# A fused transformer kernel on one core: own start and end for the feed-forward stages, SBUF pools that wait tile by tile, another load order

## The chip, the cores and the metric

The kernel runs as one launch on one NeuronCore of a Trainium2 chip. The metric is the device time of one execution in microseconds (us), taken as the median of several runs. One further execution is recorded by the hardware profiler, and all durations below come from that recording. Engines are named as in the profile: PE is TensorE, PEld its weight loads, DVE is VectorE, ACT is ScalarE, POOL is GpSimd, SP is SyncE, which here only issues DMAs.

## What is computed

The kernel works on x of 8 x 256 x 128 floats (2048 tokens of width 128) and adds six sublayers to it in turn, each on a layernorm of x:

```python
x = x + 0.5 * ffn(layernorm(x))          # a graph of six attention nodes, see below
x = x + attn(layernorm(x))               # 16 heads of 64, rotary, softmax
x = x + 0.5 * ffn(layernorm(x))          # the same graph and weights again
x = x + 0.5 * experts(layernorm(x))      # 8 experts, top 2
x = x + mixer(layernorm(x))              # two state-space scans and an FFT branch
x = x + 0.5 * experts(layernorm(x))

def ffn(inputs):
    nodes = {-1: inputs}
    for c in range(6):                   # each node reads up to five earlier ones
        q = ew[c, 0] * (nodes[c - 1] @ We[eq] + be[eq])
        k = ew[c, 1] * (nodes[s] @ We[ek] + be[ek])
        v = ew[c, 2] * (nodes[m] @ We[ev] + be[ev])
        o = mha(q, k, v, Wq[c], Wk[c], Wv[c], Wo[c])     # 8 heads of 16
        nodes[c] = act_w[c] * o + q
    return layernorm(nodes[5], ln_g, ln_b)
```

The change lies in the two `ffn` stages and in how they join their neighbours.

## The kernel before

**Stages.** In the profiled execution the first feed-forward stage takes the time from 0 to about 458 us, the attention to 810 us, the second feed-forward stage to 1244 us, the experts and the mixer the rest. The 2048 tokens are four chunks of 512 columns (`CT`), each of four tiles of 128 rows; `x[0]` to `x[3]` stay in SBUF all the time.

**Feed-forward.** `ffn()` makes 48 items out of it (`N`): six nodes, times four chunks, times the two halves (256 tokens, one batch entry) of a chunk. The eight heads of an item stand in two groups `g` of four; the four heads of a group have their own 32 rows of the TensorE array, called row tiles here. An item n goes through these steps:

- `project` (PE L290, ACT copy `qkraw` L294, four POOL operations `qk` L298): queries and keys of all heads.
- plain `scores` (PE L342): the scores are made a first time, and DVE takes their negative row maximum (`negmax`, L350) out of PSUM.
- `shift`: DVE turns the maxima into rows (`turned`, L366), and eight small DMAs, four for each group, put them into spare rows of `qk` (L372, issued by SP). With those rows the second product gives scores minus their row maximum.
- shifted `scores` (the same L342): ACT takes the exponential out of PSUM (`ex`, L355).
- `project_values` (L317, copy L326), `values` (32 matmuls `pc`, L385, and a DVE transpose `tp`, L393), `divide` (DVE `rec` L404, POOL `cn` L406), `context` (DVE L419), `output` (PE L429 to L448).
- For the last node, `output` and `close` add the layernorm and the sum into x: DVE `y` L453, statistics L82/L83, POOL L85/L87 (`ln_ve`, `ln_rs`), DVE `yn` L93, POOL `yn`*g L466, `x`+b L467, `x`+`yn` L468.

**The order.** Inside `ffn` the order of the instructions on PE, DVE, ACT and POOL is the order of the program (`manual_schedule`). One loop `for i in range(-6, N + 4)` is the software pipeline; iteration i works on seven items at once: plain scores of item i+2, shifted scores of item i, `project(i + 4)`, `project_values(i + 1)`, `output(i - 3)`, `divide` and `context(i - 2)`, `values(i - 1)`, and `shift(i + 1)` at its top. For each group it makes the scores in two bursts, `low` and `high`: `low` has two plain heads and the other two shifted heads, `high` the reverse, so that a burst uses four row tiles and four PSUM banks. In the first iterations (i below 0) only the plain half of each burst exists, in the last (i = 46 and 47) only the shifted half. Then a burst uses two row tiles.

**PSUM.** Eight banks, one tile per bank at a time, named by hand: bank 6 also holds `pc`, bank 3 also holds the two halves of `pn` (values and output), banks 0, 1 hold `pt` and others. A tile that is made in a bank waits for the readers of the tile that was there.

**SBUF.** Each stage opens its own pool (`ffn`, `attn`, `mamba`, and the weights' `w_ffn`, `w_attn`, `ffn_raw`, `w_mixer`). In the kernel before, these pools are made without `reuse_waits="tile"`: the first use of a new pool waits until everything in the pool that held the space is done. The PSUM pools have it already.

**Beside.** Small steps of other stages are woven into the loop at given iterations (`beside`): `compose(c)` folds the edge weights of node c into the projections (PE L190/L191, DVE L193, POOL L198 to L204), eight iterations ahead of use; the first layernorms of the attention and of the experts are there too. `start(ch)` is the layernorm of chunk ch (DVE L82/L83, POOL L85/L87, DVE `xn` L93, PE `pt` L129, ACT `node_in` L131); it is a generator, advanced one step per iteration.

Of the kernel before, what the change touches and what calls it, by code (L numbers as in the profile page):

```python
# [135 lines left out]
class FfnWeights:  # L136
# [5 lines left out]

    def __init__(self, nc, pool, raw, ident, cols, ins):
        self.nc, self.raw, self.ident, self.cols = nc, raw, ident, cols
        shapes = {
            "qk": [P, NODES, 2, P],
            "v": [P, NODES, P],
            "res": [P, NODES, P],  # L150
            "o": [P, NODES, P],
            "bqk": [P, NODES, 2, 2],
            "bv": [P, NODES],
            "bres": [P, NODES],
            "bres_row": [P, P],
            "g": [P, P],
            "b": [P, P],
        }
        self.w = w = {n: pool.tile(v, F32, name="w_" + n) for n, v in shapes.items()}

        w["mask"] = mask = pool.tile([P, 2], F32, name="head_rows")
        self.ones = ones = pool.tile([P, 2], F32, name="ones_rows")
        for g in range(2):
            nc.vector.tensor_reduce(
                mask[:, g : g + 1],
                ident.rearrange("p (j s d) -> p s j d", s=2, d=FD)[:, g],
                AX.XY,
                ALU.add,
            )
            nc.vector.reduce_sum(ones[:, g : g + 1], ident[:, FD * (1 - g) :: 32], axis=AX.X)  # L170
        self.ins = {
            "weT": raw.tile([P, NODES, 3, P], F32, name="weT"),
            "wqk": raw.tile([P, NODES, 2, P], F32, name="wqk_raw"),
            "wv": raw.tile([P, NODES, P], F32, name="wv_raw"),
            "weq": w["res"],
            "wo": w["o"],
        }
        for part in (slice(0, 1), slice(1, NODES)):
            for i, (name, t) in enumerate(self.ins.items()):
                queue = nc.scalar if i == 1 and part.start == 0 else nc.sync  # L180
                queue.dma_start(out=t[:, part], in_=ins["ffn_" + name][:, part])

    def compose(self, ps, c):

# [11 lines left out]
        for g in range(2):  # L196
            dst = w["bqk"][:, c, :, g]
            nc.gpsimd.tensor_scalar(dst, pb[:, 0:2], w["mask"][:, g : g + 1], None, ALU.mult)  # L198
            nc.gpsimd.tensor_tensor(dst[:, 1:2], dst[:, 1:2], self.ones[:, g : g + 1], ALU.add)
        nc.gpsimd.tensor_copy(w["bv"][:, c : c + 1], pb[:, 2:3])  # L200
        act = self.cols[:, COLS["act_w"]][:, c : c + 1]
        for v, scale in ((w["res"][:, c], ew[:, 0:1]), (w["o"][:, c], act)):
            nc.gpsimd.tensor_scalar(v, v, scale, None, ALU.mult)
# [44 lines left out]
        return self.ps.tile(shape, dtype, tag=f"bank{k}", bufs=1, name=name)  # L248


def ffn(nc, tc, ident, nhalf, x, w, first, beside):

    with ExitStack() as ctx:
        ps = psum(ctx, tc)
        pool = ctx.enter_context(tc.tile_pool(name="ffn", bufs=2))
        shifts = []
        for i in range(3):
            z = pool.tile([P, 2, 32], F32, name=f"negmax{i}", bufs=1)
# [66 lines left out]
            state[n][2] = va  # L325
            return lambda: nc.scalar.copy(va[:, :, :, 0:FD], pp)  # L326

        def scores(a, b, g, ja, jb, banks):

            todo = []  # L330
            for j in range(2):
                for n, j0, k in ((b, jb, banks[1][j]), (a, ja, banks[0][j])):
                    if not 0 <= n < N:
                        continue
                    st = state[n]
                    sc = bank(k, [P, 2, S], "sc")
                    lhs, rhs = (st[0], st[1]) if n == a else (st[1], st[0])
                    r = slice(32 * (j0 + j), 32 * (j0 + j) + 32)
                    todo.append((n, j0 + j, sc, lhs[r, g], rhs[r, g]))
            for t in range(2):  # L340
                for _, _, sc, lhs, rhs in todo:
                    nc.tensor.matmul(  # L342
                        sc[:, t, :], lhs[:, t * P : (t + 1) * P], rhs, start=True, stop=True
                    )

            def read():
                for n, j, sc, _, _ in todo:
                    if n == a:
                        sh = state[n].setdefault("sh", shifts[n % 3])
                        nc.vector.tensor_reduce(  # L350
                            sh[:, :, 4 * g + j], sc, AX.X, ALU.max, negate=True
# [5 lines left out]

            return read

        def shift(n):  # L360

            if not 0 <= n < N:
                return
# [2 lines left out]
            nc.vector.transpose(  # L366
                turned.rearrange("p t r -> p (t r)"), st["sh"].rearrange("p t c -> p (t c)")
            )
            for g in range(2):
                to = st[0][FD * (1 - g) :: 32, g, :].rearrange("p (t b r) -> p b t r", b=4, r=32)  # L370
                for b in range(4):
                    nc.sync.dma_start(  # L372
                        out=to[:, b], in_=turned[32 * b + 4 * g : 32 * b + 4 * g + 4]
                    )

# [45 lines left out]
        def output(n, pn):  # L421
# [28 lines left out]
            y = pool.tile([P, 2, D], F32, tag="y", name="y")  # L450

            def read():
                nc.vector.tensor_tensor(y, pn, bcast(w["bres_row"], 2), ALU.add)  # L453
                last.append((y, x[ch][:, 2 * b : 2 * b + 2, :], ln_stats(nc, pool, nhalf, y, 1e-6)))

            return read

# [2 lines left out]
        def close():  # L460

            while last:
                y, xs, stats = last.pop(0)
                yn = pool.tile([P, 2, D], F32, tag="yn", name="yn")
                ln_apply(nc, y, yn, *stats)
                nc.gpsimd.tensor_tensor(yn, yn, bcast(w["g"], 2), ALU.mult)  # L466
                nc.gpsimd.tensor_tensor(xs, xs, bcast(w["b"], 2), ALU.add)  # L467
                nc.gpsimd.tensor_tensor(xs, xs, yn, ALU.add)  # L468

        starts = {}  # L470
        for f in beside.get(None, ()):
            f(spare, 1)
        node[0][-1] = first
        if first is None:
            for _ in start(0):
                pass
        engines = mybir.EngineType
        ordered = {engines.PE, engines.DVE, engines.Activation, engines.Pool}
        with tc.manual_schedule(engines=ordered):
            for i in range(-6, N + 4):  # L480
                divide(i - 2)
                shift(i + 1)
                low = scores(i + 2, i, 0, 0, 2, ((0, 1), (2, 3)))
                high = scores(i + 2, i, 0, 2, 0, ((4, 5), (6, 7)))
                low()
                high()
                close()
                qk = project(i + 4)
                both = bank(3, [P, 2, S], "pn")
# [2 lines left out]
                va()  # L492
                out()
                context(i - 2)
                low = scores(i + 2, i, 1, 0, 2, ((0, 1), (6, 7)))
                high = scores(i + 2, i, 1, 2, 0, ((4, 5), (2, 3)))
                low()
                for f in beside.get(i, ()):
                    f(spare, 1)
                for ch in range(1, NCH):  # L500
                    if 2 * ch - 8 <= i:
                        if ch not in starts:
                            starts[ch] = start(ch)
                        next(starts[ch], None)
                high()
                values(i - 1)
            close()

# [23 lines left out]
def attention(nc, tc, ident, nhalf, x, cols, brow, w, first, beside):  # L532
# [9 lines left out]


    with ExitStack() as ctx:
        pool = ctx.enter_context(tc.tile_pool(name="attn", bufs=2))
        ps = psum(ctx, tc)

        sel = pool.tile([P, P], BF16, name="sel", bufs=1)
# [268 lines left out]
def experts_and_mixer(nc, tc, ident, nhalf, x, cols, ins, w, given, store):  # L817
# [17 lines left out]
    fft_b = cols[:, COLS["fft_b"]]  # L835
    UNITS, LOW = 32, DR + 2 * DS
    with ExitStack() as ctx:
        pool = ctx.enter_context(tc.tile_pool(name="mamba", bufs=1))
        ps = psum(ctx, tc)


# [810 lines left out]
def tile_kernel(ctx: ExitStack, tc: tile.TileContext, ins, out):  # L1652
# [30 lines left out]
        "gate": cpool.tile([P, NT, E, 1], F32, name="gate0"),  # L1683
    }

    with tc.tile_pool(name="w_ffn", bufs=1) as fp:
        hand = [given["xT"], *(fp.tile([P, CT], F32, name=f"first{i}") for i in (1, 2))]
        tiles = [h.rearrange("p (t d) -> p t d", t=NT) for h in hand]
        brow = fp.tile([P, P], F32, name="brow")
# [21 lines left out]
        def for_attention(ps, bufs):  # L1711
            return attention_first(nc, fp, ps, nhalf, ident, x[0], cols, brow, *hand, bufs)

        def for_ffn(ps, bufs):
            return ffn_first(nc, fp, ps, nhalf, ident, x[0], tiles[1], hand[0], bufs)

        def for_experts(ps, bufs):
            scales = ln_scales(nc, fp, nhalf, x[0], 1e-5)
# [7 lines left out]
            yield  # L1726
            expert_gates(nc, fp, eg, given["gate"])

        with tc.tile_pool(name="w_attn", bufs=1) as wp:
            with tc.tile_pool(name="ffn_raw", bufs=1) as raw:  # L1730
                made = FfnWeights(nc, fp, raw, ident, cols, ins)
                for ch in range(1, NCH):
                    nc.sync.dma_start(out=x[ch], in_=ins["x"][:, ch * NT : (ch + 1) * NT, :])
                w_moe = load(cpool, ("gate", "w1", "w3", "w2"), "m_")
                w_attn = load(wp, ("q", "k", "v", "o", "cos", "sin"), "a_")
                beside = steps(for_attention, 44, 45, 46, 46, 47, 48, 49)
                for c in range(NODES):
                    i = 8 * c - 8
                    beside.setdefault(i if c else None, []).append(
                        lambda ps, _, c=c: made.compose(ps, c)  # L1740
                    )
                    beside.setdefault(i + 1 if c else -3, []).append(
                        lambda ps, _, c=c: made.close(ps, c)
                    )
                beside.setdefault(35, []).append(lambda ps, _: made.rows(ps))
                beside.setdefault(36, []).append(out_bias)
                ffn(nc, tc, ident, nhalf, x, made.w, None, beside)
            beside = steps(for_ffn, 28, 29, 30)
            attention(nc, tc, ident, nhalf, x, cols, brow, w_attn, hand[2], beside)
        ffn(nc, tc, ident, nhalf, x, made.w, hand[0], steps(for_experts, 46, 47, 48, 49, 50))  # L1750
    with tc.tile_pool(name="w_mixer", bufs=1) as wp:
        names = ("inT", "inK", "xproj", "dtT", "sel", "FT", "ysel", "outT", "G")
        w = load(wp, names, "s_")
        w["conv"] = wp.tile([P, 2, 5, 2 * DI], F32, name="w_conv")
# [126 lines left out]
```

## Time and profile before

| | us |
|---|---|
| median of 3 runs | 1972.39 (1969.65 to 1975.15) |
| profiled execution | 1971.64 |
| its span in the trace | 1969.9, mean granted TensorE clock 0.982 |
| PE busy | 1860.1 (94%) |
| DVE busy | 1503.3 (76%) |
| POOL busy | 1074.3 (55%) |
| ACT busy | 1019.3 (52%) |
| an iteration of the feed-forward loop, in the middle | 8.19 |

The table is of the whole span. The page also cuts the span into 40 slices of about 49 us, and the trace can be asked for any stretch of it; a change of the stages' ends is to be read there. Where a row gives an engine's idle time with an arrow, the name after the arrow is the instruction whose end let it go on.

### The profile page before, as it was taken

Reading aid. Unit: us, or ns where it says so; the run is one execution under the profiler, and the core shown is the slowest. Engines: PE = TensorE matmul, PEld = TensorE weight load, DVE = VectorE, ACT = ScalarE, POOL = GpSimd, SP = SyncE. Lnnn points to the kernel's source line nnn. Section 1 sums busy time; section 2 is a strip of 40 time slices with the busy share of each in tenths; the row PEclk is TensorE's granted clock in tenths of the full one; section 3 lists DMA queues with packets and bytes.
Section 4 is the critical chain, followed back from the end, with each engine's and each line's share of the span. In section 5 each row is a group of like instructions: output and inputs, shape, how many; then the busy total and the mean of one; then the engine's idle time right before and its main releaser. Section 6 shows DMA issues by size and latency. Waiting matters only on the chain. (4 is left out here: it accounts for less than half of the span.)

```text
span 1969.9 us, 45628 instructions
## 1 busy us (share of the span) xinstructions
PE 1860.1 (94%) x17792; PEld 1143.3 (58%) x17792; DVE 1503.3 (76%) x2573; ACT 1019.3 (52%) x1911; POOL 1074.3 (55%) x1399
## 2 busy tenths in 40 slices
PE   6999999998999999899999999799989999989888
PEld 5777777764565666577777776453344344345345
DVE  5777777787878777577777777647997887997874
ACT  2666666662333222166666666445555654654544
POOL 4333333357666655433333334644878787787864
PEclk9999999998999999899999999999999999999899
DMA  4000000000000000000000000321000010000000
GB/s 151 3 3 3 3 3 3 3 3 1 2 2 2 2 2 2 1 3 3 3 3 4 3 3 3 113 72 26 12 22 22 0 30 15 12 21 12 0 1 22
DMA packets 21242, 29.27 MB, mean 15 GB/s; under 512 B 12506, under 2 KB 13914, under 8 KB 20260
## 3 DMA queue, kind: packets, MB, share of 16 engines
q1 hardware_dynamic: 20740, 26.15, 4.5%
q8 instruction: 142, 2.33, 0.5%
q14 instruction: 72, 0.59, 0.1%
q10 hardware_dynamic: 288, 0.20, 0.0%
HBM read 16.10 MB, written 1.05 MB: 9 GB/s over the span
## 5 line engine op out<-in xcount | busy, mean ns | idle before, releaser
L350 DVE TENSOR_REDUCE negmax<-sc 128x2 f32<-128x512 f32 x768 | 475.0, 677 | 126.7 <-PE sc L342 126.4
L355 ACT ACTIVATE ex<-sc 128x512 f32<-128x512 f32 x768 | 398.0, 603 | 231.9 <-PE sc L342 231.9
L342 PE MATMUL sc<-qk,qk 32*128 32x256 f32 x6144 | 423.1, 397 | 8.0 <-DVE tp L393 2.7
L342 PEld LDWEIGHTS sc<-qk,qk 32*128 32x128 f32 x6144 | 309.8, 187 | 109.7 <-issue 65.5
L1219 POOL TENSOR_TENSOR hc<-h,C 128x1024 f32<-128x1024 f32 x128 | 301.3, 2357 | 112.0 <-DVE h L1217 106.9
L298 POOL TENSOR_SCALAR qk<-qkraw,head_rows,w_bqk 128x256 f32<-128x256 f32 x384 | 207.8, 555 | 203.8 <-ACT qkraw L294 197.8
L1217 DVE TENSOR_TENSOR_SCAN h<-dA,pU 128x1024 f32<-128x1024 f32 x128 | 292.1, 2282 | 13.4 <-POOL hc L1219 0.9
L406 POOL TENSOR_TENSOR cn<-tp,rec 128x256 f32<-128x256 f32 x96 | 59.5, 620 | 287.1 <-DVE rec L404 287.1
L1199 ACT ACTIVATE dA<-p,cols 128x512 f32<-128x512 f32 x256 | 162.1, 684 | 102.8 <-PE p L1197 100.6
L1206 DVE TENSOR_TENSOR pU<-pU,B 128x1024 f32<-128x1024 f32 x128 | 155.7, 1216 | 59.0 <-PE p L1197 51.8
L385 PE MATMUL pc<-ex,va 128*32 128x256 f32 x3072 | 185.7, 382 | 0.3 <-ACT ex L355 0.3
L639 ACT ACTIVATE ex<-sc 128x512 f32<-128x512 f32 x128 | 66.1, 603 | 204.5 <-PE sc L624 204.5
L1197 PE MATMUL pU<-du,s_sel 32*128 32x512 f32 x512 | 146.4, 645 | 19.5 <-DVE h L1217 14.0
L1197 PE MATMUL p<-dl,s_sel 32*128 32x512 f32 x512 | 154.2, 635 | 4.3 <-ACT dA L1199 4.2
L624 PE MATMUL sc<-rot,rot 32*128 32x256 f32 x2048 | 135.2, 388 | 0.3 <-POOL rot L607 0.3
L385 PEld LDWEIGHTS pc<-ex,va 128*32 128x32 f32 x3072 | 90.0, 109 | 78.1 <-ACT ex L355 28.0
L642 POOL TENSOR_TENSOR both<-ex 128x512 f32<-128x512 f32 x64 | 80.0, 1271 | 71.7 <-ACT ex L639 71.7
L624 PEld LDWEIGHTS sc<-rot,rot 32*128 32x128 f32 x2048 | 97.9, 184 | 35.1 <-issue 22.6
L634 DVE TENSOR_REDUCE anegmax<-sc 128x2 f32<-128x512 f32 x128 | 79.4, 683 | 22.1 <-PE sc L624 22.1
L1197 PEld LDWEIGHTS pU<-du,s_sel 32*128 32x128 f32 x512 | 40.3, 185 | 89.6 <-issue 65.2
L393 DVE STREAM_TRANSPOSE tp<-pc 128x512 f32<-128x512 f32 x96 | 68.6, 715 | 28.0 <-PE pc L385 28.0
L1010 POOL TENSOR_TENSOR sg_hT<-sg_hT,hid 128x512 f32<-128x512 f32 x32 | 40.5, 1267 | 65.9 <-ACT sg_hT L1009 65.9
(293 smaller groups left out, 3098.7 us busy)
## 6 DMA issues: line engine op xcount, KB each, us to landing
qk<-turned SPq DMA_DIRECT2D x768, 1.0 KB
s_fft<-s_fft SPq DMA_DIRECT2D x5, 1024.0 KB
du<-ab SPq DMA_DIRECT2D x16, 256.0 KB
B<-low SPq DMA_DIRECT2D x64, 32.0 KB
C<-low SPq DMA_DIRECT2D x64, 32.0 KB
x<-x SPq DMA_DIRECT2D x4, 256.0 KB
s_inK<-s_inK SPq DMA_DIRECT2D x1, 1024.0 KB
out<-x SPq DMA_DIRECT2D x4, 256.0 KB
```

The source lines that it names most:

```text
L298: nc.gpsimd.tensor_scalar(t[:, g, :], raw[:, i, :], w["mask"][:, g : g + 1], w["bqk"][:, c, i, g : g + 1], ALU.mult, ALU.add,)
L342: nc.tensor.matmul(sc[:, t, :], lhs[:, t * P : (t + 1) * P], rhs, start=True, stop=True)
L350: nc.vector.tensor_reduce(sh[:, :, 4 * g + j], sc, AX.X, ALU.max, negate=True)
L355: nc.scalar.activation(ex, sc, AF.Exp, scale=FD**-0.5)
L385: nc.tensor.matmul(st["pc"][32 * j : 32 * j + 32, g, :], st[2][:, kt, 2 * j + g, :], st["ex", g, j][:, kt, :], start=(kt == 0), stop=(kt = ...
L624: nc.tensor.matmul(sc[j][:, t, :], lhs[r, part, t * P : (t + 1) * P] if part < 2 else sel[r, :], rhs[r, part, :] if part < 2 else st["nm"] ...
L642: nc.gpsimd.tensor_tensor(both, ex[:, :, 0], ex[:, :, 1], ALU.add)
L1197: nc.tensor.matmul(dst, w["sel"][rs, i, :], src[rs, :], start=True, stop=True)
L1199: nc.scalar.activation(dA, pA, AF.Exp, scale=rate)
L1206: nc.vector.tensor_tensor(dB, dB, bcast(gots[ch]["B", r], 2), ALU.mult)
L1217: nc.vector.tensor_tensor_scan(hf, af, bf, 0.0, ALU.mult, ALU.add)
L1219: nc.gpsimd.tensor_tensor(hc, h, bcast(gots[ch]["C", r], 2), ALU.mult)
```

## The change

In words:

1. **Own prologue.** `first_maxima()` takes the place of the iterations below 0. It makes the plain scores of items 0 and 1 with `alone(n, g, False, banks)`: four heads of one group in one burst on four row tiles. The maxima of item 0 are turned per group, and their DMAs are issued in turn by SP and by ACT. The layernorms of chunks 1 to 3 stand at set places between these; the last step of chunk 3 (`pt`, `node_in`) comes at i = 1. The POOL operations that scale `w_res`, `w_o` and `w_bres` of node 0 are split off as `scale(0)` and stand behind `project(3)`.
2. **Own epilogue.** For i = 46 and 47 the four shifted heads of a group are one burst: banks (6, 7, 2, 3) for group 0, (2, 3, 6, 7) for group 1. A head's bank is the same as before. The iterations between have the order and banks of before.
3. **`x` + b** (L467 before) moves from `close` to `output`, ahead of the item's own statistics.
4. **Second feed-forward stage.** The layernorm of chunk 1 is made during the attention (slots 21 to 23, beside that of chunk 0 in slots 28 to 30).
5. **Pools.** All seven SBUF pools get `reuse_waits="tile"`.
6. **Loads.** Chunk 1 of x is fetched behind the weights of node 0 and ahead of the other feed-forward weights, chunks 2 and 3 behind them.

The core of the diff:

```diff
@@ FfnWeights.__init__, compose @@
+            if part.start == 0:
+                between()
...
+        if c:
+            self.scale(c)
+    def scale(self, c):
...
@@ ffn @@
-        pool = ctx.enter_context(tc.tile_pool(name="ffn", bufs=2))
+        pool = ctx.enter_context(tc.tile_pool(name="ffn", bufs=2, reuse_waits="tile"))
...
+        def pair(i, g):
+            a, b = ((0, 1), (4, 5)), (((2, 3), (6, 7)), ((6, 7), (2, 3)))[g]
+            for k in range(2):
+                heads = []
+                for j in range(2):
+                    heads.append((i, (2, 0)[k] + j, True, b[k][j]))
+                    heads.append((i + 2, (0, 2)[k] + j, False, a[k][j]))
+                yield scores(g, *heads)
+
+        def alone(n, g, shifted, banks):
+            return scores(g, *((n, j, shifted, k) for j, k in enumerate(banks)))
+
-        def shift(n):
+        def shift(n, gs=(0, 1), queues=(nc.sync, nc.sync)):
...
-                    nc.sync.dma_start(
+                    queues[b % 2].dma_start(
...
             def read():
+                xs = x[ch][:, 2 * b : 2 * b + 2, :]
+                nc.gpsimd.tensor_tensor(xs, xs, bcast(w["b"], 2), ALU.add)
                 nc.vector.tensor_tensor(y, pn, bcast(w["bres_row"], 2), ALU.add)
...
                 nc.gpsimd.tensor_tensor(yn, yn, bcast(w["g"], 2), ALU.mult)
-                nc.gpsimd.tensor_tensor(xs, xs, bcast(w["b"], 2), ALU.add)
                 nc.gpsimd.tensor_tensor(xs, xs, yn, ALU.add)
+        def first_maxima():
+            made = [] if firsts else [start(0)]
+            if made:
+                next(made[0])
+                next(made[0])
+            for f in beside.get("compose", ()):
+                f(spare, 1)
+            if made:
+                next(made[0], None)
+                made.append(start(1))
+                next(made[1])
+            project(0)()
+            if made:
+                next(made[1])
+            project(1)()
+            alone(0, 0, False, (4, 5, 6, 7))()
+            shift(0, (0,), (nc.sync, nc.scalar))
+            if made:
+                next(made[1], None)
+            project(2)()
+            alone(0, 1, False, (3, 0, 1, 4))()
+            shift(0, (1,), (nc.sync, nc.scalar))
+            project(3)()
+            for f in beside.get("scale", ()):
+                f(spare, 1)
+            starts[2] = start(2)
+            next(starts[2])
+            alone(1, 0, False, (5, 6, 7, 3))()
+            project_values(0, bank(2, [P, S], "pn"))()
+            next(starts[2])
+            next(starts[2], None)
+            alone(1, 1, False, (0, 1, 4, 5))()
+            starts[3] = start(3)
+            next(starts[3])
...
-            for i in range(-6, N + 4):
+            first_maxima()
+            for i in range(N + 4):
                 divide(i - 2)
                 shift(i + 1)
-                low = scores(i + 2, i, 0, 0, 2, ((0, 1), (2, 3)))
-                high = scores(i + 2, i, 0, 2, 0, ((4, 5), (6, 7)))
-                low()
-                high()
+                if i + 2 < N:
+                    reads = list(pair(i, 0))
+                else:
+                    reads = [alone(i, 0, True, (6, 7, 2, 3))] if i < N else []
+                for f in reads:
+                    f()
...
+                if i + 2 < N:
+                    reads = list(pair(i, 1))
+                else:
+                    reads = [alone(i, 1, True, (2, 3, 6, 7))] if i < N else []
...
-            beside = steps(for_ffn, 28, 29, 30)
+            beside = steps(for_ffn(1), 21, 22, 23) | steps(for_ffn(0), 28, 29, 30)
```

## The prediction

> **What bounds the kernel now.** First the page, for the whole span:
>
> ```profile
> PE 1860.1 (94%) x17792; PEld 1143.3 (58%) x17792; DVE 1503.3 (76%) x2573; ACT 1019.3 (52%) x1911; POOL 1074.3 (55%) x1399
> PE   6999999998999999899999999799989999989888
> PEclk9999999998999999899999999999999999999899
> ```
>
> PE fills the slices, and in the feed-forward stages what is not PE sits at their ends: slices 0, 9, 16, 25. (A digit hides stretches under 49 us.) So, second, busy time by stretch; the columns are length, then PE, PEld, DVE, ACT, POOL busy (instructions), granted clock, DMA share, GB/s:
>
> ```profile
> 30.00:40.00 10.00, 9.52 (x53) 6.80 (x56) 6.15 (x15) 0.96 (x2) 3.44 (x6) 0.66 0.01 2
> 830.00:845.00 15.00, 14.00 (x97) 9.88 (x95) 7.73 (x16) 5.23 (x11) 4.32 (x8) 0.68 0.01 1
> 860.00:1200.00 340.00, 339.82 (x4493) 243.59 (x4486) 267.31 (x504) 223.38 (x456) 115.61 (x208) 1.00 0.02 3
> 1220.00:1235.00 15.00, 13.18 (x156) 9.04 (x144) 9.27 (x30) 6.67 (x14) 10.10 (x19) 1.00 0.01 1
> ```
>
> In the middle PE is busy without a gap at full clock, 8.19 us an iteration, and the change leaves that order alone: it is costed at nothing. In the prologues PE gets five instructions per us against thirteen, at a clock of two thirds; at the epilogues it waits (13.18 of 15). Third, the timeline at the first epilogue, i = 46 (start, length, what ran, idle before it):
>
> ```profile
> 431.06 1.13 PE L342 MATMUL sc<-qk,qk 32*128 32x256 f32 x8
> 432.28 1.08 ACT L355 ACTIVATE ex<-sc 128x512 f32<-128x512 f32 x2 [1.36 <-PE sc L342]
> 432.42 0.70 DVE L393 STREAM_TRANSPOSE tp<-pc 128x512 f32<-128x512 f32 x1
> 433.18 1.13 PE L342 MATMUL sc<-qk,qk 32*128 32x256 f32 x8 [0.98 <-DVE tp L393]
> 434.24 0.71 PE L317 MATMUL pn<-w_v,node 128*128 128x128 f32 x4
> 434.34 1.08 ACT L355 ACTIVATE ex<-sc 128x512 f32<-128x512 f32 x2 [0.97 <-PE sc L342]
> 435.77 2.12 PE L342 MATMUL sc<-qk,qk 32*128 32x256 f32 x16
> 437.82 1.93 PE L385 MATMUL pc<-ex,va 128*32 128x256 f32 x32
> ```
>
> The first `sc` (heads 2, 3, banks 2, 3) runs and is exponentiated while `tp` empties bank 6; only the second (heads 0, 1) waits. `pn`, in bank 3, follows at once because bank 3 was read early. Fourth, the waits at the two places where a new SBUF pool opens (engine and line, what it waited for, total, times, longest):
>
> ```profile
> DVE ropecos L601 <- POOL x L468: 2.3, 1, 2.3
> ...
> DVE hid L1006 <- POOL x L468: 2.3, 1, 2.3
> ...
> DVE s_inK L872 <- DMA s_inK<-s_inK: 1.6, 1, 1.6
> ```
>
> **The change, part by part** (line numbers of before).
>
> *Pools.* `ropecos` reads PSUM and writes a new tile; x is not its operand, so its 2.3 us and those of `hid` are the pool's wait. Both go. At the attention's start POOL's constants (464.62 to 466.55, 2.0 us) still follow x, and `rot` (466.55) follows them; so 2.3 there is the most. The mixer's loads start about 14 us earlier (`s_inT` waited until 1245.35, and needs only the end of `pt`, 1230.9), but of them the path shows just the 1.6 us of `s_inK`; I count nothing for it, bound −1.6.
>
> *Epilogues.* Four heads in one burst begin with head 0, bank 6, which holds `pc`: nothing starts before `tp` ends at 433.18. The four tiles take about 1.1 us (the middle has 2.05 for an x32 pair of bursts), the four `ex` 2.16 (twice 1.08): 434.3 to 436.5. Head 3 is in bank 3 and is read last, so `pn` starts at 436.5, not 434.24: +2.2. Its matmuls end 1.5 later at 438.0, `y` (0.42 after a 0.5 latency) frees bank 3 at 438.9. Group 1 has head 1 in bank 3, its second matmul, where before heads 2, 3 went first in banks 6, 7 at 435.77; now it ends at 440.0. `pc` needs bank 6, that is head 2, the third `ex`: 440.0 + 3 x 0.54 = 441.6 against 437.82: **+3.8**. Iteration 47 repeats it: `tp` at 444.4, burst to 445.6, four `ex` to 447.7, `pn` +5.8, `pc`(46) at 452.3 against 444.95, **+7.4**. Then there are no scores; `pc`(47) follows at +7.1 and the last `y` at about **+6.9** (before: 458.17). Nothing covers this: DVE, ACT and POOL wait for the same chain. Moving `x`+b takes one POOL operation (0.72) from behind the last `yn`; both later consumers then hang on DVE, not on x. Attention start: 6.9 − 2.3 = +4.6 by `ropecos`, +6.2 by `rot` (6.9 − 0.7); I take **+5.0**, as the second `rot` waits for DVE. Mixer start: the same walk from 1214.55 gives `hid` at 1250.25 against 1245.35: **+4.9**. Bounds for each: −3 (no delay, 2.3 and 0.7 gained) to +7.
>
> *First prologue.* Gains: x chunk 0 lands at 4.56, but its `ln_rs` stood behind the scaling operations on POOL (0.61 + 0.62 + 0.19) and the wait for `compose`; now `xn` is at 7.5 instead of 13.33, `pp` of item 0 at about 10 instead of 15.64, and item 0's first plain scores at 15.1 instead of 21.53. Losses: ACT issues two of each group's four DMAs, and the issue waits for `turned` (about 19.5, after four `negmax` at 0.62). Queued behind it on ACT are `node_in` of chunk 1 (19.71 before, 20.5 now) and later `qkraw` of item 3; PE has `pp` of item 2 ahead of group 1's scores, so these wait too. On POOL, `qk` of item 3 (2.2), `scale(0)` (1.4) and `ln_rs` of chunk 2 come in this order, the latter at 33 to 35; PE has chunk 2's `pt` ahead of the last plain burst of item 1, which thus starts at 36 to 39. `negmax` and chunk 3's statistics (eight operations, 1.8) follow, and `turned` of item 1 is made at 41.7 to 44, against 41.86. So 6 us won at the head are lost behind ACT and POOL: **+1.0**, from −3 (full clock throughout) to +4 (clock 0.66 as in the row above).
>
> *Second prologue.* Here both chunks are ready and `qk` of item 0 no longer stands behind a layernorm:
>
> ```profile
> 811.91 0.58 ACT L294 COPY qkraw<-pp 128x512 f32<-128x512 f32 x1 [11.47 <-PE pp L290]
> 812.66 1.04 POOL L87 TENSOR_TENSOR ln_rs<-ln_ve,nhalf 128x4 f32<-128x4 f32 x1
> 813.70 2.27 POOL L298 TENSOR_SCALAR qk<-qkraw,head_rows,w_bqk 128x256 f32<-128x256 f32 x4
> ```
>
> −1.1 at `qk`, the pair of i = 0 at about 831.6 instead of 833.89, and by i = 2 at 849 instead of 853.80 if the clock holds: **−3.5** (−6 to 0).
>
> *Moved layernorm.* PE's part lies in the PE-bound attention: four `pt`, 0.66: **+0.6**; DVE's (1.8 + 1.1) and POOL's (1.3) lie beside it. Bounds 0 and +2.
>
> *Sum*: 5.0 + 4.9 + 1.0 − 3.5 + 0.6 = +8.0. On the profiled execution's 1971.64 that is 1979.6, say **1980**; the median is 0.75 above that execution, which I leave in the rounding.
>
> Around the two-tile bursts PE idles 0.98 and ACT 1.36, and a burst of two tiles (1.13) takes as long as one of four (2.05 for two): PE's rate is not what the epilogue waits for. The Trainium skill, TensorEngine Tiling (Array Packing), Theoretical Speedup, says that a dimension of at most 32 can be packed four tiles at a time for up to four times the speed; read as a gain of time, each of the four epilogue iterations would save two bursts, 9 us in all, and the sum would be about −15 (1957), an estimate from that page. I go by the rows. The skill's DMA: Bandwidth & Descriptors, Issuing engines are not separate DMA queues, speaks against the split of the issues: it saves the sequencer's issuing time alone; no run here shows that yet.
>
> **Rivals.** *Faster: the epilogues cost little.* The steps outside them sum to −1.9 (1.0 − 3.5 + 0.6), and the released waits are worth 1.9 (6.9 − 5.0) and 2.0 (6.9 − 4.9). Let E be the delay of a last `y`: the total is 2E − 3.9 − 1.9. Below E = 2.9 the kernel gains; at E = 0 with the prologues at their good ends (−4 and −2.5 more) it stands at 1971.6 − 12.3, about 1959, and at 1966 without. For it: the first `pn` and `pc` after the burst might not be what the last `y` hangs on. Against: `tp` and `ex` in the rows. Chance 0.27. *Nothing measurable:* E near 3, or a full clock in both prologues against my epilogues: 1966 to 1978; chance 0.23. It comes about too if the first prologue keeps its 6 us. *Slower still:* the ACT queue and the slow clock cost both prologues their gains (+3, +3.5): 1986 to 1990; chance 0.1. *My forecast*, 1978 to 1986: 0.40. That the change does not do what it says is no case here: the middle is the same order by construction, and of the early loads only 1.6 us ever showed.
>
> **How the numbers follow.** About 0.3%, 5.9 us, is what a measurement of this kernel can tell from no change. Faster by more than that: 0.27; within: 0.23; slower: 0.50. The range reaches from 1960, near the lower end of the faster case, to 1989; my own case alone has 1975 to 1986.
>
> **What would show it.** Right: in i = 46 the four `sc` begin after `tp`, `pn` after the fourth `ex`; last `y` of stage one near 465; `ropecos` without a pool wait, near 469; `hid` near 1253 (1245.35 and the sum). Wrong: `y` under 461; item 0's shifted scores before 37; an iteration in the middle other than 8.19; a clock near 1 in 30 to 40.

## The result, and the profile after

The changed kernel takes 2001.38 us (median of 4 runs, 1995.93 to 2003.32) against 1973.77 before; the ratio is 1.013, with a 95% interval from 1.0091 to 1.017. It is slower, by more than three times the 8 us of the forecast, and above its range. The profiled execution took 1999.93 us, its span is 1998.1. The page of after, the same three lines:

```profile
PE 1866.8 (93%) x17792; PEld 1144.5 (57%) x17792; DVE 1505.0 (75%) x2575; ACT 1019.6 (51%) x1911; POOL 1074.4 (54%) x1399
PE   6999999987999999899999998799999999989888
PEclk8999999998999999999999998899999999999999
```

The busy times hardly moved: PE has 6.6 us more for the same 17792 instructions (that is a slower clock, 0.970 against 0.982 in the mean, not more work), and the span has 28.2 more. So the question is where PE waits and where it runs slowly, and that is read by following one instruction that exists in both traces:

| the same instruction | before | after | later by | step |
|---|---|---|---|---|
| `y` of item 40, first stage | 410.63 | 414.93 | 4.3 | first prologue +4.3 |
| `y` of item 47, first stage | 458.17 | 475.78 | 17.6 | first end **+13.3** |
| first `nm` of the attention | 479.37 | 496.12 | 16.7 | pools and start −0.9 |
| last `x` of the attention | 810.22 | 829.31 | 19.1 | moved layernorm +2.3 |
| `y` of item 40, second stage | 1193.60 | 1208.52 | 14.9 | second prologue −4.2 |
| `y` of item 47, second stage | 1238.62 | 1267.18 | 28.6 | second end **+13.6** |
| first `hid` of the experts | 1245.35 | 1271.51 | 26.2 | pool wait −2.4 |
| end of the span | 1969.9 | 1998.1 | 28.2 | experts and mixer +2.0 |

(`y` is one item's sum in DVE, `nm` the turned row maxima of the attention, written by ACT.) The middle of the loop is not in it: from item 3 to item 46 of the first stage the `turned` of an item comes 4.3 later than before, without change. The two ends of the feed-forward stages make 26.9 of the 28.2. I call the time from the `y` of item 40 to that of item 47 the closing stretch: 47.5 and 45.0 us before, 60.9 and 58.7 after.

The timeline of after at the first end, i = 46; the columns are start, length, what ran, and idle time before it:

```profile
437.47 1.77 PE L348 MATMUL sc<-qk,qk 32*128 32x256 f32 x16 [2.04 <-DVE tp L413]
439.29 2.06 ACT L361 ACTIVATE ex<-sc 128x512 f32<-128x512 f32 x4 [4.08 <-PE sc L348]
441.41 1.22 PE L326 MATMUL pn<-w_v,node 128*128 128x128 f32 x4 [2.17 <-ACT ex L361]
444.27 2.13 PE L348 MATMUL sc<-qk,qk 32*128 32x256 f32 x16
447.73 3.34 PE L405 MATMUL pc<-ex,va 128*32 128x256 f32 x32 [1.33 <-ACT ex L361]
```

The order of waits is the one forecast: the burst begins behind `tp`, `pn` behind the fourth `ex`, `pc` behind the third `ex` of the second group. But look at the lengths. The matmuls `pc` take 3.34 us, and in the next iteration 3.64, for the 1.93 of before; `pn`'s first four take 1.22 for 0.71. The busy time by stretch gives the reason (length, then PE, PEld, DVE, ACT, POOL busy with their instructions, granted clock, DMA share, GB/s):

```profile
420.00:435.00 15.00, 14.03 (x196) 10.16 (x192) 14.56 (x39) 9.31 (x20) 8.30 (x16) 1.00 0.02 4
435.00:440.00 5.00, 2.19 (x24) 0.98 (x16) 3.51 (x11) 0.92 (x3) 3.53 (x8) 0.79 0.00 0
440.00:445.00 5.00, 3.59 (x14) 3.11 (x14) 0.22 (x1) 1.73 (x4) 1.02 (x2) 0.53 0.01 1
445.00:450.00 5.00, 3.56 (x42) 1.90 (x45) 2.08 (x10) 2.82 (x6) 2.29 (x6) 0.81 0.01 3
450.00:455.00 5.00, 2.21 (x28) 0.91 (x20) 1.75 (x4) 1.95 (x4) 2.56 (x4) 0.84 0.00 0
455.00:460.00 5.00, 4.68 (x24) 3.56 (x24) 1.59 (x6) 0.77 (x3) 1.12 (x3) 0.50 0.00 0
460.00:465.00 5.00, 3.93 (x33) 1.75 (x34) 1.06 (x5) 2.71 (x7) 1.36 (x4) 0.50 0.00 0
```

Asked for in single us, the granted clock is 1.00 up to 437, 0.50 from 438 to 444, 1.00 from 445 to 448, 0.50 from 449 to 451, 1.00 from 452 to 454 and 0.50 from 455 to 465. In the slow stretches the matmuls on the chain took up to twice as long. The forecast counted the waits and left the clock at 1. That the waits brought the clock down is a theory here; the experiments test it.

### The profile page after: what moved, and what is told of

Read it like the earlier page. It is cut to its first block, busy times and chain, and to the rows that moved or that the text cites. A ratio compares the mean times of both kernels' runs of the same rounds, so it can differ in the third digit from the quotient of the medians.

```text
span 1998.1 us, 45623 instructions
## 1 busy us (share of the span) xinstructions
PE 1866.8 (93%) x17792; PEld 1144.5 (57%) x17792; DVE 1505.0 (75%) x2575; ACT 1019.6 (51%) x1911; POOL 1074.4 (54%) x1399
## 4 chain that ended last, share of the span: by engine, by line
PE 77%; DVE 11%; POOL 5%; ACT 4%; issue 2%; ACTq 0%; DMA 0%; DVEq 0%; POOLq 0%
PE sc L348 18%; PE pc L405 9%; PE sc L681 7%; PE pp L299 5%; PE pU L1254 5%; DVE h L1274 4%; PE pc L740 3%; PE p L1139 3%; PE pp L652 3%; PE p L1337 2%; PE pn L326 2%; PE p L1254 2%; DVE negmax L356 2%; PE ph L1058 2%; PE pn L449 2%
## 5 line engine op out<-in xcount | busy, mean ns | idle before, releaser
L348 PE MATMUL sc<-qk,qk 32*128 32x256 f32 x6144 | 418.4, 401 | 9.7 <-DVE tp L413 6.5
L405 PE MATMUL pc<-ex,va 128*32 128x256 f32 x3072 | 192.2, 392 | 5.0 <-ACT ex L361 5.0
```

The lines of the kernel that those rows point to most:

```text
L348: nc.tensor.matmul(sc[:, t, :], lhs[:, t * P : (t + 1) * P], rhs, start=True, stop=True)
L405: nc.tensor.matmul(st["pc"][32 * j : 32 * j + 32, g, :], st[2][:, kt, 2 * j + g, :], st["ex", g, j][:, kt, :], start=(kt == 0), stop=(kt = ...
```

## Experiments

Theory A: the four-head bursts sit in banks that something else holds (bank 6 `pc`, bank 3 `pn`), this costs about 7 us an end, and the gaps let the clock fall, which costs about 6 more. Rivals: the pools or the moved sum do it; the clock is beside the point; four shifted heads at once are bad in themselves. Beside the ends, three smaller steps were tried alone: ACT's DMA issues, the moved layernorm, the pools.

### The old end in the changed kernel

```diff
-                    reads = [alone(i, 0, True, (6, 7, 2, 3))] if i < N else []
+                    reads = list(halves(i, 0)) if i < N else []   # heads 2, 3, then 0, 1, banks of before
```

> The changed kernel with the old end of the feed-forward stages: for i = 46 and 47 two bursts of two heads (2, 3, then 0, 1) in the old banks. Closing stretch = from the y of item 40 to the y of item 47: 47.5 us (first stage) and 45.0 (second) before, 60.9 and 58.7 after. Theory A (the four-head bursts wait for bank 6 and hold bank 3, and the gaps let the clock fall): both stretches return to 47 to 48 and 45 to 46, the granted clock there to about 1, the execution is 25 to 28 us shorter than the changed kernel's, near 1973. Rival B (the moved x+b or the tile-by-tile pools lengthen the ends): the stretches stay at 58 to 61 and the time within 5 us of the changed kernel's 2000.

1975.84 us, ratio to before 1.0025 (1.0009 to 1.0041): 25.5 us less than the changed kernel. The closing stretches are 49.0 and 45.0. So the bursts of the end are the loss, and rival B falls but for 1.45 us in the first stage. These lie where the clock is low in this trace, 0.57 from 438 to 442, and `pn`'s matmuls take 0.63 a pair instead of 0.39. Before has 1.00 from 430 to 442, with the same idle time of 0.98 on PE ahead of the second burst.

### PE kept busy at the end, twice

```diff
+        def warm(n):
+
+            spent = bank(4, [P, 2, P], "spent")
+            for _ in range(n):
+                nc.tensor.matmul(spent, ident, w["qk"][:, 0, :, :], start=True, stop=True)
...
+                        warm(3)      # ahead of group 0's burst; 1 in the second kernel
...
+                        warm(7)      # ahead of pn; 4 in the second kernel
...
+                        warm(4)      # ahead of pc; 2 in the second kernel
```

> The changed kernel, and in i = 46 and 47 fourteen extra matmuls of 128 x 256 each iteration, on resident data into bank 4, which is idle there and is never read: three ahead of group 0's burst, seven ahead of pn, four ahead of pc. They fill PE's waiting, they shorten no dependency. Theory A (of the 13.3 us that the closing stretch grew by, 7 are the waits themselves and 6 are PE at a granted clock of 0.5): the clock stays near 1, pc takes 1.9 instead of 3.6, and the stretches are 54 to 56 and 52 to 54, the execution 10 to 13 us shorter than the changed kernel's. Rival C (the clock is beside the point, the chain through tp, ex and y takes this long by itself): the stretches stay at 60 and 58 or grow by what the extra matmuls take.

> As the kernel with extra matmuls at the stage's end (changed kernel otherwise), with half as many: one, four and two instead of three, seven and four. There the clock was 1.00 throughout, but the extra matmuls ran past the end of the wait by about 2.7 us in all (pn 0.9 late twice, the burst 0.3 and 0.6), and the stretches were 57.6 and 55.1. Theory A (waits 7, clock 6): the clock stays at 1 or little below, and the stretches are 54 to 55.5 and 52 to 53.5. Rival C (the clock adds nothing): 57 or more, as the waits alone make it; or, if half as many do not hold the clock, pc at 3 us and more and the stretches near 60.

With the many matmuls: stretches 57.6 and 55.1, above the 54 to 56 and 52 to 54 expected, ratio 1.0134 (1.0097 to 1.017). The clock was 1.00 there, but the extra work ran past the waits, so this kernel does not separate the two theories. With half of them: 54.3 and 51.6, ratio 1.008 (1.0065 to 1.0096). The busy time by stretch of that second kernel, at the same place:

```profile
435.00:440.00 5.00, 4.73 (x38) 3.66 (x34) 0.95 (x4) 2.29 (x5) 2.75 (x4) 1.00 0.01 1
440.00:445.00 5.00, 4.43 (x53) 2.34 (x51) 2.31 (x10) 2.96 (x7) 2.29 (x6) 1.00 0.02 4
450.00:455.00 5.00, 4.73 (x56) 2.76 (x54) 2.36 (x10) 2.82 (x6) 0.93 (x2) 1.00 0.00 0
```

and two lines of its timeline:

```profile
438.13 0.71 PE L326 MATMUL pn<-w_v,node 128*128 128x128 f32 x4 [0.27 <-ACT ex L361]
443.13 1.93 PE L411 MATMUL pc<-ex,va 128*32 128x256 f32 x32 [0.27 <-ACT ex L361]
```

`pn` and `pc` still wait for the same `ex`, so no dependency became shorter; useless work was added, and the two stretches became 13.5 us shorter together than in the changed kernel (its median is 12.7 lower). The clock stood at 1.00 from 425 to 460 and `pc` took 1.93. This shows the clock's share: 60.9 − 54.3 = 6.5 us in the first end, 58.7 − 51.6 = 7.0 in the second. What is left against before, 54.3 − 47.5 = 6.8 and 51.6 − 45.0 = 6.6, is the waits. Against the old end in the changed kernel it is 5.3 and 6.6; the first is smaller because that old end has lost 1.45 to the clock itself.

### The bursts in free banks

```diff
-                    reads = [alone(i, 0, True, (6, 7, 2, 3))] if i < N else []
+                    reads = [alone(i, 0, True, ((0, 1, 7, 2), (7, 2, 4, 5))[i % 2])] if i < N else []
...
-                    reads = [alone(i, 1, True, (2, 3, 6, 7))] if i < N else []
+                    reads = [alone(i, 1, True, ((4, 5, 0, 1), (0, 1, 7, 2))[i % 2])] if i < N else []
```

> The changed kernel, four heads in one burst as it has them, but in banks that nothing else holds at the end of the stage: (0, 1, 7, 2) and (4, 5, 0, 1) in i = 46, (7, 2, 4, 5) and (0, 1, 7, 2) in i = 47, so neither tp in bank 6 nor pn in bank 3 is in the way. Theory A (banks): the bursts start at once, the clock stays near 1, the closing stretches are 43 to 48 and 41 to 46, at or below before's, and the execution is 25 to 34 us shorter than the changed kernel's, 1966 to 1975. Rival D (four shifted heads at once are bad in themselves, as ACT gets sixteen exponentials in a row and PE nothing else): stretches of 52 or more, clock below 0.8.

1974.26 us, ratio 1.0014 (0.9997 to 1.0031); stretches 45.0 and 41.7, 2.6 and 3.3 *below* before. Its timeline at i = 46:

```profile
432.57 1.15 PE L348 MATMUL sc<-qk,qk 32*128 32x256 f32 x16
433.65 0.71 PE L326 MATMUL pn<-w_v,node 128*128 128x128 f32 x4
433.80 2.06 ACT L361 ACTIVATE ex<-sc 128x512 f32<-128x512 f32 x4 [1.36 <-PE sc L348]
435.18 1.15 PE L348 MATMUL sc<-qk,qk 32*128 32x256 f32 x16
436.26 1.93 PE L405 MATMUL pc<-ex,va 128*32 128x256 f32 x32
```

Nothing on PE has an idle time before it; `ex` runs beside `pn`, the next burst and `pc`. Four shifted heads at once are not bad at all (rival D falls); the banks were. The profiled execution, with 1965.57, is 6 us below before's 1971.64. The median is not below before's: three of the ten executions take 1966, seven 1970.9 to 1976.2, and what makes these longer no trace shows.

### One bank at a time

```diff
-(6, 7, 2, 3) and (2, 3, 6, 7)
+(1, 7, 2, 3) and (2, 3, 1, 7)      # without bank 6
+(6, 7, 2, 1) and (2, 1, 6, 7)      # without bank 3
```

> The changed kernel with one bank changed in the last two iterations: the head that shared bank 6 with pc goes to bank 1, which is free; bank 3 is still shared with pn. Stretch from the y of item 40 to that of item 47: 60.9 and 58.7 in the changed kernel, 47.5 and 45.0 before, 45.0 and 41.7 with both banks free. Theory A1 (the two shared banks make the delay together: without bank 6 the burst starts beside tp and pc no longer waits for the third ex, only pn waits for the fourth): 47 to 50 and 45 to 48, clock near 1. Rival J (bank 3, which holds pn back by the whole row of exponentials, makes the delay alone): 55 and more.

> The other half: the head that shared bank 3 with pn goes to bank 1, bank 6 is still shared with pc. Theory A1: pn follows the burst at once, the second group's burst waits for no y, only the burst behind tp and pc behind the third ex remain: 47 to 51 and 45 to 49, clock near 1. Rival K (bank 6 makes the delay alone): 55 and more.

Without bank 6: 51.1 and 46.6 us, total ratio 1.004 (1.0028 to 1.0052). Without bank 3: 51.5 and 49.0, ratio 1.0027 (1.0015 to 1.0038). The first stretches lie 1.1 and 0.5 us over the ranges given, since the clock still falls late, where it was expected near 1: without bank 3 it is 0.87 and 0.78 from 440 to 450; without bank 6 it is 1.00 until 445 and then

```profile
445.00:450.00 5.00, 2.88 (x29) 2.17 (x25) 2.19 (x7) 2.32 (x5) 2.99 (x5) 0.87 0.00 0
450.00:455.00 5.00, 5.00 (x47) 2.31 (x42) 1.65 (x8) 2.92 (x6) 1.15 (x3) 0.50 0.00 0
```

Against the old end in the changed kernel (49.0 and 45.0), bank 3 alone costs 2.1 and 1.6, bank 6 alone 2.5 and 4.0, both together 11.9 and 13.6. Together they cost far more than the sum (4.6 and 5.6). With the clock held at 1.00 by the extra matmuls they cost 5.3 and 6.6, near the sum; the rest is the clock.

### The free banks in the kernel before

The edit of the free banks, put into the old loop's last two iterations.

> The kernel before with one edit: in its last two iterations of each feed-forward stage the four shifted heads of a group are one burst in free banks (0, 1, 7, 2), (4, 5, 0, 1), (7, 2, 4, 5), (0, 1, 7, 2). If the gain of that end is its own, the stretches are 45.0 and 41.7 instead of 47.5 and 45.0 and the kernel is 4 to 6 us faster than before, 0.2 to 0.3%. Rival: the pool's wait at the attention's and mixer's start hangs on the last sum into x and swallows part of it: 0 to 3 us.

1965.71 us, ratio 0.9958 (0.9942 to 0.9974); stretches 45.0 and 41.7. The median is 6.8 us below before's, so the 5.9 us of the two stretches are not lost again further on. The repaired end is a gain by itself, 0.4%.

### SP alone issues the DMAs of the new prologue

```diff
-            shift(0, (0,), (nc.sync, nc.scalar))
+            shift(0, (0,), (nc.sync, nc.sync))
```

> The changed kernel, with all four DMAs of a group in the new prologue issued by SP, as before, instead of two by SP and two by ACT. Theory E (ACT, waiting to issue, holds back node_in of chunk 1 and qkraw of item 3): node_in of chunk 1 at 17.9 instead of 21.5, group 1's scores of item 0 at 20 instead of 24.2, turned of item 1 at 40 to 42 instead of 43.8, the loop in the middle 2 to 4 us earlier in the first stage and 1 to 2 in the second. Rival (ACT's blocking costs nothing, POOL's scaling and chunk 2's layernorm set item 1's second burst): turned of item 1 within 1 us of 43.8, and the time unchanged.

Three lines of after's timeline, then three of this kernel's:

```profile
19.71 1.75 ACTq L392 DMA_DIRECT2D qk<-turned  x2
21.51 0.58 ACT L131 COPY node_in<-pt 128x512 f32<-128x512 f32 x1 [6.14 <-DMA qk<-turned]
22.14 2.07 PE L299 MATMUL pp<-node_in,w_qk 128*128 128x256 f32 x4 [4.34 <-ACT node_in L131]
```

```profile
17.94 0.59 ACT L131 COPY node_in<-pt 128x512 f32<-128x512 f32 x1 [2.48 <-PE pt L129]
18.58 2.07 PE L299 MATMUL pp<-node_in,w_qk 128*128 128x256 f32 x4 [0.68 <-ACT node_in L131]
20.58 2.09 PE L348 MATMUL sc<-qk,qk 32*128 32x256 f32 x16
```

ACT had copied `pt` 3.6 us late because it stood waiting to issue; PE and the second group's scores followed. Without that, `turned` of item 1 comes at 37.3 instead of 43.8 (41.9 before), and the `y` of item 40 at 408.4 instead of 414.9. The whole is 1991.34 us, ratio 1.0119 (1.0094 to 1.0144). Its median is 10 us below the changed kernel's and its trace 9 us shorter, but the interval of the ratio overlaps the changed kernel's (1.0091 to 1.017), so the total alone does not show the gain; the instants do. The effect is larger than forecast: `scale(0)` and chunk 2's layernorm on POOL, next in line, move with it (`w_res` is scaled at 26.7 instead of 33.2). The kernels with SP's issues put this `y` at 403.3 to 408.4 (three traces), those with ACT's issues at 412.2 to 415.3 (seven), those with the old prologue at 408.8 to 413.0 (four): ACT's issues turned a gain of some 5 us into a loss of some 3. A part of this goes through the clock. From 20 to 100 us it is 0.87 in the changed kernel and 0.91 here; the same code in two later kernels has 0.96, and this `y` at 403.3 and 403.7 instead of 408.4.

### Chunk 1's layernorm back in the second stage

```diff
-            beside = steps(for_ffn(1), 21, 22, 23) | steps(for_ffn(0), 28, 29, 30)
+            beside = steps(for_ffn(0), 28, 29, 30)
...
-        ffn(nc, tc, ident, nhalf, x, made.w, hand[::2], steps(for_experts, 46, 47, 48, 49, 50))
+        ffn(nc, tc, ident, nhalf, x, made.w, hand[:1], steps(for_experts, 46, 47, 48, 49, 50))
```

This stands on the kernel with both repairs (free banks, SP's issues), which is the last of this section.

> As the kernel with both repairs, but the layernorm of chunk 1 for the second stage is made in that stage's own prologue again, and not in the attention. Theory F (the moved layernorm costs the attention 2.35 us, because DVE's four xn take 3.3 us beside POOL's rot there, and brings the second prologue 4): the attention (from the first nm to the last x) takes 330.9 instead of 333.2, the way from that x to the y of item 40 becomes 2 to 5 us longer, and the kernel is 0 to 3 us slower than the one with both repairs. Rival G (the move is a loss): 1 to 3 us faster.

1957.09 us, ratio 0.993 (0.9911 to 0.9948), the same as with the move (0.9933). The attention, from the first `nm` to the last `x`, takes 330.86 instead of 333.22, and the way from there to item 40's `y` 380.41 instead of 377.95: 2.4 lost, 2.5 won. A move of no worth, since in the attention DVE pays for it, as theory F has it; the total, 2.0 us below in the median with overlapping intervals, does not tell F from G. After's timeline there:

```profile
722.39 3.32 DVE L93 TENSOR_SCALAR first<-x,ln_mv,ln_rs 128x128 f32<-128x128 f32 x4
722.86 1.28 POOL L665 TENSOR_TENSOR rot<-ropecos,ropesin 128x512 f32<-128x512 f32 x1
724.09 1.28 POOL L664 TENSOR_TENSOR rot<-ropecos,ropesin 128x512 f32<-128x512 f32 x1
725.63 2.47 DVE L691 TENSOR_REDUCE anegmax<-sc 128x2 f32<-128x512 f32 x4
```

The four operations take 3.32 us beside POOL's two `rot`, against 1.1 in the prologue where POOL was idle (at 7.60), and the row maxima of the attention are queued behind them.

### The pools alone, and with the moved sum

```diff
-        pool = ctx.enter_context(tc.tile_pool(name="ffn", bufs=2))
+        pool = ctx.enter_context(tc.tile_pool(name="ffn", bufs=2, reuse_waits="tile"))   # and the six others
```

> The kernel before with reuse_waits="tile" on its seven SBUF pools and nothing else. By the prediction: ropecos begins 2.3 us earlier and the attention as a whole 0.7 to 2.3, hid 2.3 earlier, the mixer's loads 14 us earlier with at most 1.6 on the path; 3 to 6 us in all, 0.15 to 0.3%. Rival H (other waits take their place, as POOL's constants still follow x and the mixer's loads were never late): under 1.5 us. Rival I (the early loads collide with the feed-forward stage's small DMAs): slower.

1978.26 us, ratio 1.0025 (1.0011 to 1.004): slower, against the forecast of 3 to 6 us less. `ropecos` came 4.02 us after the last `y` instead of 6.42 and `hid` 4.3 instead of 6.7, as forecast. But the first scores of the attention came 14.98 after it instead of 15.14, and took longer:

```profile
471.30 3.80 PE L624 MATMUL sc<-rot,rot 32*128 32x256 f32 x32 [2.94 <-POOL rot L607]
```

They wait for POOL (last sums into x, constants, `rot`), which the pools do not touch; PE idled 2.9 us in front of them, and they ran at little over half speed (2.01 before): the clock is 0.50 from 470 to 475. The first `nm` is 1.6 later than before. With the moved sum added:

```diff
+                nc.gpsimd.tensor_tensor(xs, xs, bcast(w["b"], 2), ALU.add)
                 nc.vector.tensor_tensor(y, pn, bcast(w["bres_row"], 2), ALU.add)
...
-                nc.gpsimd.tensor_tensor(xs, xs, bcast(w["b"], 2), ALU.add)
```

> The kernel before with tile-by-tile SBUF pools, as measured alone (there the first scores of the attention came 14.98 us after the last y instead of 15.14, but took 3.8 us instead of 2.0, and the first nm came 22.83 after it instead of 21.20), and in addition x+b moved ahead of the item's statistics, as in the changed kernel. Theory L (POOL's queue sets the start: x, constants, rot; one sum of 0.72 less in front of them): first scores 14.3 and first nm 20.35 after the last y, as in the changed kernel. Rival (something else of the changed kernel made its start quicker): 14.98 and 22.8 as with the pools alone.

```profile
473.34 2.01 PE L625 MATMUL sc<-rot,rot 32*128 32x256 f32 x32 [2.70 <-POOL rot L608]
```

First scores at 14.32, first `nm` at 20.38, as in the changed kernel; 1970.91 us, ratio 0.9984 (0.9968 to 1.0001). Theory L holds for the first scores. Of the 2.45 us at `nm`, 1.8 are the scores' own time (3.80 to 2.01), at a clock of 1.00 after nearly the same idle time, 2.7 us; that is not the sum's doing as far as the traces show. The first closing stretch is 49.0 instead of 47.5, as in the first experiment, and here too the clock is low in it, 0.52 from 434 to 437.5. The second stage has the same moved sum and 45.0, as before, so that the sum costs anything at the end is not shown.

The rest of the loss with the pools alone lies behind the stages: at the last `y` its trace is still 4.0 us ahead of before's, and from there to the end it takes 738.8 us, against 731.3 before and 731.4 with the same pools and the sum. PE is busy for 674.2, 665.7 and 667.5 us of this way with the same 3112 matmuls, at a mean clock of 0.96, 0.98 and 0.97. It is a slower clock, and as the same pools have it in one trace and not in the other, I don't put it on them.

### Both repairs

> The changed kernel with both repairs: the four-head bursts at the stage's end in free banks, and the new prologue's DMAs issued by SP alone. If the two are independent: y of item 40 near 408 (410.6 before), closing stretches 45 and 41.7, the second stage as in the changed kernel, the execution 1957 to 1963 against 1971.6 before, 0.4 to 0.7% faster. Rival: what is won at the first prologue is lost again where the attention starts or in the mixer, and the time stays within 0.3% of before.

1959.1 us, ratio 0.9933 (0.9915 to 0.9952): 0.7% faster than before, 42 us less than the changed kernel. `y` of item 40 at 403.3, stretches 45.0 and 41.7. With chunk 1's layernorm left in its stage it is as fast (0.993 against 0.9933), so the move can be left out.

## Why the forecast was wrong, point by point

*The ends, +6.9 each in the last `y`, bounds −3 to +7: the step that failed.* They measured +13.3 and +13.6. What failed is the length of the matmuls behind the waits: the walk took 1.5 for `pn`'s (2.9 measured, 441.41 to 444.27) and 1.93 for `pc` (3.34), durations of rows where PE was never idle, and the sum has no term for a slower clock. That term measured 6.5 and 7.0. The waits were where the walk put them, and together as long: with the clock held at 1.00 the stretches are 6.8 and 6.6 above before's, for the 6.9 of the walk. Less the 1.6 us by which that kernel's `y` of item 40 comes later than before's, its `pn` starts at 436.5 (forecast 436.5), `pc` at 441.5 (441.6) and the last `y` at 464.9 (465.1). For the prologues I had read the clock of 0.66 beside gaps in the trace of before and put it into the bounds; for the ends I had not, though the walk itself opened gaps of 2 us there, and though the trace of before has 0.50 from 455 to 460, in the last us of the stage. The upper bound of +7 was the walk itself, and so the range ended too low: 13 of the 20 us between 1980 and the measured execution come from here.

On this clock the Trainium skill, TensorE: Matmul & The Clock Gate, HAM oscillation — how this bites in real kernels, says that the array falls to half rate when a gap in PE's work outlasts some 3.4 us. Here the longest gaps of the end are 2.0 and 2.2 us, and the clock fell to 0.50; the measurement decides: shorter gaps are enough. The first fall, at 438, came behind a single gap of 2.0 (435.4 to 437.5). But in the kernel without bank 3 the same gap of 2.04, ahead of a burst at 437.56, left the clock at 1.00 up to 443, and the old end's gap of 0.98 had a fall near it in two traces and none in before's. So the length of one gap does not tell whether the clock falls; what does was not measured.

*First prologue, +1.0 from −3 to +4*: +4.3, just above its bound. The walk's instants held up to item 1: `xn` 7.60 (forecast 7.5), first scores 14.67 (15.1), `node_in` of chunk 1 21.51 (20.5), last plain burst 37.48 (36 to 39), `turned` of item 1 43.80 (41.7 to 44); the clock was 0.66 to 0.75 from 20 to 40, which was the upper end. At item 1's `turned` the kernel is 1.9 us behind before; the other 2.4 come by item 3, where the walk had stopped and the clock is 0.57 from 52 to 60. That ACT's issues were the reason is shown by the kernel without them, whose `y` of item 40 is ahead of before's.

*Second prologue, −3.5*: −4.2. *Moved layernorm, +0.6, bounds 0 to +2*: +2.3; I had costed PE's part and let DVE's lie beside, at the duration it has with POOL idle; the trace of before has the same four operations for chunk 0 in the attention, at 776.39, with 3.00. *Pools*: 2.3 each at `ropecos` and `hid` as forecast, but the attention's start gained 0.9 and not 1.9, since `rot` on POOL and not `ropecos` set it (there the first scores move with POOL's queue, by 0.66 for one sum of 0.72). *Mixer's loads*: nothing, as counted; the first scan starts 113 to 116 us after the last `y` in every trace.

*The rivals.* The faster case (E near 0) asked that the banks not matter; they do, and the free banks show that the case was one edit away. The slower case named the wrong place, the prologues.

## What to carry to other kernels

When a walk through a changed order opens gaps on PE, redo it with PE's work behind the gaps at the lowest clock that the trace shows near other gaps; a wait can be paid once as idle time and once more as slow matmuls, here 6.8 and 6.5 us in the first end. When work is packed wider, give it buffers that nothing else holds at that moment: in free banks the packing was worth 3 us an end, in shared banks it cost 13. And don't let an engine that others wait for issue a DMA whose data isn't ready yet.

## What was not expected of the hardware

- The granted clock fell to 0.50 with no gap on PE longer than 2.2 us, and it stayed there through 5 us without a gap (450 to 455 in the kernel without bank 6: PE busy 5.00, clock 0.50). Filling the gaps with unused matmuls kept it at 1.00 and took 13.5 us off the two stretches.
- DVE's `xn`, four operations, took 3.3 us beside POOL's `rot` and 1.1 beside an idle POOL (7.60 in after's trace). The attention's row maxima are not slowed by the same `rot`: 2.48 beside two of them in the trace of before (at 706.41), 2.47 without (at 725.63 after).
- The time of the experts and the mixer differs by up to 10 us between traces (729 to 739 us from the last `y` to the end), more than most steps of this study. The four longest (735 to 739) have PE busy for 669 to 674 us of it, the ten others (729 to 733) for 663 to 668, with the same matmuls: it goes with the clock. Only instants followed through the trace could tell the steps apart.
